# First layer's local attention: a fixed TensorE order in turns 3 to 11, taps in pairs, and 32x32 transposes for norms and reciprocals

## The chip, the cores and the metric

The kernel runs on one core of a Trainium2 chip. The metric is the device time of one execution in microseconds. The engines are called PE (TensorE), DVE (VectorE), ACT (ScalarE), POOL (GpSimd) and SP (the queue that issues all DMAs here); PEld is PE's weight load. All data is fp32.

## The reference

Four image layers are applied to two images of 512 channels and 64x64 pixels, each after a group norm and with a residual. The change lies in the first, a local-plus-pooled attention with 8 heads of 64 channels:

```python
q_norm = _l2norm(q)                                   # per token and head
q_scaled = (q_norm + query_embedding) * softplus(temperature)
k_l = _l2norm(k_l)
attn_local = einsum('bhnd,bhndk->bhnk', q_scaled, k_local)   # 3x3 neighbours: 9 taps
attn_pool = einsum('bhnd,bhpd->bhnp', q_scaled, _l2norm(k_pool))   # 256 pooled keys
attn = softmax(concatenate([attn_local, attn_pool], axis=-1), axis=-1)
a_local, a_pool = attn[..., :9], attn[..., 9:]
lt = einsum('bhnd,hdk->bhnk', q_norm, learnable_tokens) + learnable_bias + a_local
x_local = einsum('bhnk,bhndk->bhnd', lt, v_local)
x_pool = einsum('bhnp,bhpd->bhnd', a_pool, v_pool)
out = (x_local + x_pool) @ W_proj + b_proj
```

## The kernel before, in words

The class `Local` (from line 1938) computes this layer for one image. Channels lie on partitions, 128 at a time, so a chunk of channels holds two heads. A unit is one chunk and 1024 tokens (16 image rows): 4 chunks by 4 blocks of tokens make 16 units. `run` (line 2018) walks through turns i = -4 to 16. One turn works on several units at once, in a software pipeline: it projects the keys of unit i+4 and the queries of unit i+3 (`projections`, line 2255), makes their norms (`norms`, line 2289), multiplies them in one turn later (`normed`, line 2333), forms the tap products and sums of unit i+1 (`tap_products` line 2379, `tap_sums` line 2394), attends for unit i (`attend`, line 2421) and weighs the values of unit i-1 with the nine local probabilities and the pooled part (`weigh`, line 2502). Each stage is a Python generator. `in_turn` runs all of them to their next `yield`, again and again, so a turn is some ten steps in which each stage contributes a piece. Which step a piece stands in fixes the order in which the program is written.

It doesn't fix the order in which the engines run it. The Tile scheduler orders each engine's instructions by priority (the written order) and by when it takes them to be ready, and places the semaphores. PE's queue therefore mixes pieces of neighbouring steps and turns.

PSUM has eight banks. Five of them are a common pool (`bank()`, name `mm`), one holds the tap sums, two hold a PSUM copy of the queries (`qs`).

What the prediction's steps touch:

- **Norms.** At line 2299 four matmuls, each with 32 output rows, sum the squares of the two heads of four streams (two key blocks, two query blocks) into one bank. Line 2302 copies it to SBUF on ACT, line 2306 transposes it on PE in four 128x128 pieces, so that tokens lie on partitions and the 32 useful numbers of a partition are short rows. Lines 2313 to 2321 form 1/sqrt on DVE by three Newton steps, 13 small instructions, into `wide`. At step 5 line 2327 transposes back on PE and line 2329 copies to SBUF. `normed` spreads the two rows of a stream over the channels with a matmul of two rows (line 2341) and multiplies on DVE (line 2349). `learned` (line 2362) then multiplies the queries with the learnable tokens.
- **Taps.** Line 2384 copies the queries to PSUM. For each of nine shifts line 2389 multiplies them with the shifted keys on DVE (128x1024) into one of three buffers, and line 2402 sums over channels on PE: per product and half of the tokens one matmul with 32 output columns, up to four of which lie side by side in the array.
- **Pooled attention.** Line 2434 makes the scores (two heads side by side, 64 rows each), line 2438 the exponentials, line 2444 the weighted pooled values, line 2449 adds the exponentials in pairs on POOL. `sums` (lines 2456 and 2460) forms the denominators at step 7 in a bank in which every row of a head holds the same sums, and line 2481 takes the reciprocal of all 128x512 in two halves on DVE. Lines 2484 and 2485 finish the local probabilities; line 2488 writes them to DRAM at step 8, and line 2500 fetches each tap's row back spread over 64 partitions.
- **Weighing.** For each of ten parts ACT copies the fetched tap into two banks (line 2514), DVE multiplies (lines 2519 and 2522), POOL adds (line 2527). Three tap buffers go round.
- **Projections.** Line 134 (`project`) does four matmuls of 128x128 by 512 for a block. A turn has six such blocks: two keys and two queries at steps 6 to 9, two values at steps 0 and 3.
- `fetch_output` loads W_proj into the four `sq` tiles in turn 13; `output` applies it in the last turns.

Of the kernel before, what the change touches and what calls it, by code (L numbers as in the profile page):

```python
# [9 lines left out]
F32 = mybir.dt.float32  # L10
I32 = mybir.dt.int32
AF = mybir.ActivationFunctionType
ALU = mybir.AluOpType
# [3 lines left out]
P = 128  # L17
# [1920 lines left out]
class Local:  # L1938
# [9 lines left out]
    def __init__(self, net, X, Y, sp_scale, d, wp, yp, pp, ppt, pps):  # L1948
# [20 lines left out]
        self.prods = [whole.take([P, self.UT])] + [new([P, self.UT], f"prod{i}") for i in range(2)]  # L1969
# [19 lines left out]
        self.qn = new([P, self.UT], "qn")  # L1989
# [3 lines left out]
        self.wide = new([P, NT, P], "wide")  # L1993
# [12 lines left out]
        nc.gpsimd.memset(self.wide, 0.0)  # L2006
# [11 lines left out]
    def run(self):  # L2018


        self.nmean = self.net.stats[:, 0]
        xs = self.pooled_tokens()
        heads = self.pooled_heads(xs)
        units = KC * self.UN
        unit = lambda u: u if 0 <= u < units else None
        self.pending = []
        for i in "qkv":
            self.fetch(i, 0)
        for i in range(-4, units + 1):
            k, q, ahead, u, before = (unit(i + n) for n in (4, 3, 1, 0, -1))  # L2030
            streams, ended = [], []
            stages = [self.norms(streams, ended)]
            if ahead is not None:
                stages.append(self.tap_products(ahead))
            if u is not None:
                stages.append(self.attend(u))
            if before is not None:
                stages.append(self.weigh(before))
            if ahead is not None:
                stages.append(self.tap_sums(ahead))  # L2040

            values = ([ahead] if i >= self.UN - 1 and ahead is not None
                      else {-4: [0], -3: [1, 2], -2: [3]}.get(i, []))
            stages.append(self.projections(k, q, values, streams))
            stages.append(self.normed(ended))
            if i < -2:
                stages.append(islice(heads, 12 if i == -4 else None))
            if i == units - 3:
                stages.append(self.fetch_output())
            if i > units - 3:  # L2050
                stages.append(self.output(i - units + 2))
            in_turn(*stages)

        self.nc.sync.dma_start(self.next_w, self.d["w_q1"].rearrange("(kc p) o -> p kc o", p=P))
        in_turn(self.output(KC - 1))
# [136 lines left out]
    def fetch_output(self):  # L2192

        for _ in range(3):

            yield
        for kc in range(KC):
            self.nc.sync.dma_start(self.sq[kc], self.d["W_proj"][kc * P:(kc + 1) * P, :])
        self.pb = self.kp[:, :2, :].rearrange("p c n -> p (c n)")
        self.nc.sync.dma_start(self.pb, self.d["pb_rows"])  # L2200
        yield

    def output(self, c4):
# [4 lines left out]
        toks = ([self.prods[0], self.prods[1], self.prods[2], self.qs[(units - 2) % 3]] if c4 % 2  # L2208
# [46 lines left out]
    def projections(self, uk, uq, uvs, streams):  # L2255
# [22 lines left out]
        values = [(u, j) for u in uvs for j in range(2)]  # L2278
        for step in range(10):
            if step >= 6:  # L2280
                project((uk, uq)[step // 2 - 3], "kq"[step // 2 - 3], step % 2)
            if step % 3 == 0 and values:
                u, j = values.pop(0)
                self.value(u, j)
                if j and self.last(u):
                    self.fetch("v", u // self.UN + 1)
            yield

    def norms(self, streams, ended):
# [11 lines left out]
        rows = wp.tile([P, TB], F32, name="n_rows")  # L2301
        nc.scalar.copy(rows, ps)
        yield
        ps = self.bank()
        for t in range(NT):
            nc.tensor.transpose(ps[:, t * P:(t + 1) * P], rows[:, t * P:(t + 1) * P],
                                self.net.ident)


        sums = ps.rearrange("p (t s r) -> p t s r", t=NT, s=4)  # L2310
        n, a = (sums[:, :, :, 2 * i:2 * i + 2] for i in range(2))
        y = wp.tile([P, NT, 4, 2], F32, name="roots")
# [4 lines left out]
        for i in range(3):  # L2317
            nc.vector.tensor_tensor(a, n, y, ALU.mult)
            nc.vector.tensor_tensor(a, a, y, ALU.mult)
            dst = self.wide.rearrange("p t (s r) -> p t s r", s=4)[:, :, :, :2] if i == 2 else y  # L2320
            nc.vector.scalar_tensor_tensor(dst, a, 1.5, y, ALU.add, ALU.mult)
        yield
        yield
        yield
        ps = self.bank()
        for t in range(NT):
            nc.tensor.transpose(ps[:, t * P:(t + 1) * P], self.wide[:, t, :], self.net.ident)
        rows = wp.tile([P, TB], F32, name="n_rows")
        nc.scalar.copy(rows, ps)
# [3 lines left out]
    def normed(self, ended):  # L2333

        nc = self.nc
        for _ in range(5):
            yield
        for which in "kq":
# [4 lines left out]
            for (_, _, _, u, j, part, _), ps in mine:  # L2343
# [5 lines left out]
                nc.vector.tensor_tensor(out, part, ps, ALU.mult)  # L2349
# [29 lines left out]
    def tap_products(self, u):  # L2379

        qs = self.pps.tile([P, self.UT], F32, name="qs")
        for j in range(2):
            part = slice(j * TB, (j + 1) * TB)
            self.nc.scalar.copy(qs[:, part], self.qs[u % 3][:, part])
        qs = qs.rearrange("p (y x) -> p y x", x=W)
        y = u % self.UN * self.UY
        for k in range(9):
            dy, dx = divmod(k, 3)
            self.nc.vector.tensor_tensor(  # L2389
                self.prods[k % 3].rearrange("p (y x) -> p y x", x=W), qs,  # L2390
                self.kx[:, y + dy:y + dy + self.UY, dx:dx + W], ALU.mult)
            yield

    def tap_sums(self, u):
# [3 lines left out]

        def sums(k):
            for j in range(2):  # L2400
                q = 2 * j + k % 2
                nc.tensor.matmul(ps[32 * q:32 * q + 32, :],  # L2402
                                 self.cst[:, C_TAPW + 16 - 2 * k:C_TAPW + 48 - 2 * k],
                                 self.prods[k % 3][:, j * TB:(j + 1) * TB], start=(k < 2),
                                 stop=(k > 6))

        yield
        yield
        for k in range(0, 8, 2):
            sums(k)  # L2410
            sums(k + 1)
            yield
            if k < 6:
                yield
        sums(8)
# [5 lines left out]
    def attend(self, u):  # L2421
# [5 lines left out]
        prob = {}  # L2427
# [12 lines left out]
        def values(j):  # L2440
# [6 lines left out]
            dst = prob[1, 1] if j else self.halves  # L2447
            for h in range(2):
                nc.gpsimd.tensor_tensor(dst[h], prob[j, 0][h], prob[j, 1][h], ALU.add)  # L2449

        def sums():
            psD = self.bank()
            blocks = [slice(j * HD, (j + 1) * HD) for j in range(2)]
            for h in range(2):
                for j, b in enumerate(blocks):
                    nc.tensor.matmul(psD[b, :], self.cst[:, C_EVEN + h:C_EVEN + h + HD],
                                     (prob[1, 1] if j else self.halves)[h], start=(h == 0),
                                     stop=False)
# [8 lines left out]
        yield  # L2467
        values(0)
        yield
        exponentials(1, 0)  # L2470
        yield
        exponentials(1, 1)
        yield
        values(1)
        yield
        yield
        psD = sums()

        for i in range(2):
            part = slice(i * TB // 2, (i + 1) * TB // 2)  # L2480
            nc.vector.reciprocal(self.recip[:, part], psD[:, part])  # L2481
# [3 lines left out]
        nc.vector.tensor_tensor(el, el, self.lt.pop(u), ALU.add)  # L2485
        self.spread = self.rows()
# [237 lines left out]
```

## Time and profile before

| | |
|---|---|
| median of three runs | 5136.01 us (5133.57 to 5157.94) |
| profiled execution | 5143.42 us, span of its instructions 5141.5 us |
| mean granted TensorE clock | 0.981 |
| PE busy | 4890.5 us, 95% |
| DVE, ACT, POOL busy | 3069.4, 1864.1, 1845.4 us |
| first layer, first image: first and last L2299 group | 196.8 and 859.6 us |
| steady turns 4 to 11, first image | 465.6 to 817.4 us |
| the same, second image | 3017.3 to 3368.3 us |
| DMA fetch of a tap row (L2500), issue to landing | 4.1 us |

An fp32 matmul is recorded as two instructions. Matmuls overlap in PE's pipeline, so the length of a record is more than its share of time: what a group costs is read from its start to the next group's start. In the waits, a line reads: who waited, for whom, total us, times, longest us. The granted clock is the share of full speed that PE's clock was given in the stretch.

### The profile page before, as it was taken

The numbers are of one execution on the slowest core, as the hardware profiler recorded it, in microseconds if no ns is written. First come the engines' busy times: TensorE is split into PE (matmuls) and PEld (weight loads), VectorE is DVE, ScalarE is ACT, GpSimd is POOL, SyncE is SP. The second block draws the span as 40 slices with busy tenths as digits, with TensorE's granted clock in tenths as the row PEclk, the third lists the DMA queues.
The fourth block names the chain that finished last, engine by engine and source line by source line (L and its number), as shares of the span: only waits on it lengthen the run. The fifth ranks groups of instructions, "written<-read, shape, count | busy, mean of one in ns | idle before, by whom it ended". The sixth has DMA issues, their size and how long they took to land. (4 is left out here: it accounts for less than half of the span.)

```text
span 5141.5 us, 48728 instructions
## 1 busy us (share of the span) xinstructions
PE 4890.5 (95%) x17299; PEld 2030.9 (39%) x17299; DVE 3069.4 (60%) x3986; ACT 1864.1 (36%) x3547; POOL 1845.4 (36%) x1216
## 2 busy tenths in 40 slices
PE   7999999899999999999999999998999999999998
PEld 3423332455334444433344333335543344444333
DVE  4267777654579633477732677777446795334766
ACT  1245665334323233322112566652343232333221
POOL 0025566500420045454500455555013201454554
PEclk9999999999999999999999999999999999999999
DMA  3025556600000000111110355565000000000111
GB/s 150 2 74 141 143 139 171 178 28 10 1 1 17 2 1 1 66 58 46 64 62 2 95 137 148 142 170 163 19 10 1 2 15 1 1 1 21 40 46 44
DMA packets 124752, 309.88 MB, mean 60 GB/s; under 512 B 20882, under 2 KB 33682, under 8 KB 122964
## 3 DMA queue, kind: packets, MB, share of 16 engines
q1 hardware_dynamic: 124500, 306.68, 20.7%
q8 instruction: 139, 2.28, 0.2%
q14 instruction: 113, 0.93, 0.1%
HBM read 258.11 MB, written 48.50 MB: 60 GB/s over the span
## 5 line engine op out<-in xcount | busy, mean ns | idle before, releaser
L134 PE MATMUL mm<-big,w 128*128 128x512 f32 x2496 | 1163.9, 611 | 8.6 <-DVE late L2481 8.6
L134 PEld LDWEIGHTS mm<-big,w 128*128 128x128 f32 x2496 | 456.4, 192 | 677.3 <-issue 560.3
L2527 POOL TENSOR_TENSOR late<-late,big 128x1024 f32<-128x1024 f32 x192 | 455.0, 2370 | 199.6 <-DVE big L2522 174.4
L1639 POOL TENSOR_TENSOR big<-big 128x512 f32<-128x512 f32 x224 | 277.5, 1271 | 219.6 <-ACT big L1630 219.6
L2449 POOL TENSOR_TENSOR late<-late 128x512 f32<-128x512 f32 x128 | 160.7, 1275 | 521.3 <-ACT late L2438 499.4
L2522 DVE TENSOR_TENSOR big<-big,mm 128x512 f32<-128x512 f32 x384 | 255.6, 681 | 119.0 <-ACT mm L2514 111.4
L2514 ACT COPY mm<-big 128x512 f32<-128x512 f32 x428 | 244.7, 593 | 170.4 <-DMA big<-rows 127.8
L1630 ACT ACTIVATE big<-mm,ed 128x256 f32<-128x256 f32 x512 | 194.0, 490 | 232.6 <-DVE top L1626 200.3
L2527 POOL TENSOR_TENSOR late<-late,tap 128x1024 f32<-128x1024 f32 x96 | 227.2, 2367 | 100.7 <-DVE tap L2522 96.2
L1442 POOL TENSOR_TENSOR wq<-prob 128x512 f32<-128x512 f32 x48 | 70.8, 1497 | 505.6 <-ACT prob L1439 505.6
L1894 PE MATMUL mm<-k,w 128*128 128x512 f32 x512 | 238.5, 610 | 12.3 <-DVE k L1887 7.4
L1626 DVE TENSOR_REDUCE top<-mm 128x1 f32<-128x512 f32 x256 | 159.0, 683 | 148.2 <-PE mm L1557 148.2
L134 PE MATMUL mm<-big,wq 128*128 128x512 f32 x512 | 233.8, 605 | 2.7 <-ACT off_t L1223 2.7
L2389 DVE TENSOR_TENSOR prod<-qs,big 128x1024 f32<-128x1024 f32 x192 | 230.4, 1215 | 8.8 <-PE tap L2402 6.6
L1604 PE MATMUL mm<-w,big 128*128 128x512 f32 x512 | 235.1, 603 | 0.0
L1195 PE MATMUL mm<-big,wo 128*128 128x512 f32 x512 | 234.7, 604 | 0.0
L1352 PE MATMUL acc<-big,diag 128*128 128x512 f32 x512 | 227.4, 601 | 4.6 <-ACT diag L1357 4.6
L973 POOL TENSOR_TENSOR group_stats<-group_stats,cst 128x1 f32<-128x1 f32 (+1 forms) x20 | 12.1, 622 | 574.4 <-DVE group_stats L972 514.2
L1884 DVE RECIPROCAL psD<-psD 128x512 f32<-128x512 f32 x64 | 215.1, 3361 | 1.9
L2402 PE MATMUL tap<-prod,cst 128*32 128x512 f32 x768 | 198.7, 603 | 8.8 <-DVE prod L2389 7.8
L134 PE MATMUL mm<-big,big 128*128 128x512 f32 x464 | 201.7, 594 | 0.5 <-DVE b_sr L1011 0.5
L1439 ACT ACTIVATE prob<-mm 128x512 f32<-128x512 f32 x256 | 133.0, 602 | 171.6 <-PE mm L1436 171.3
(410 smaller groups left out, 8466.1 us busy)
## 6 DMA issues: line engine op xcount, KB each, us to landing
big<-rows SPq DMA_DIRECT2D x428, 256.0 KB, 4.1
tap<-rows SPq DMA_DIRECT2D x212, 256.0 KB, 4.1
yd<-late SPq DMA_DIRECT2D x32, 512.0 KB, 2.9
lost_all<-lost SPq DMA_DIRECT2D x128, 128.0 KB, 3.0
out<-big SPq DMA_DIRECT2D x64, 256.0 KB, 2.0
big<-in_W_kv SPq DMA_DIRECT2D x8, 1024.0 KB, 8.1
rows<-late SPq DMA_DIRECT2D x64, 128.0 KB, 2.3
big<-yd SPq DMA_DIRECT2D x16, 512.0 KB, 5.2
```

Of the source, the lines that this page charges most:

```text
L134: self.nc.tensor.matmul(ps, w[:, kc, :], X[:, kc, blk * TB:(blk + 1) * TB], start=(kc == 0), stop=(kc == KC - 1))
L1195: nc.tensor.matmul(ps, w[:, kc, oc * P:(oc + 1) * P], att[:, kc, :], start=(kc == 0), stop=(kc == KC - 1))
L1352: nc.tensor.matmul(accs[b], dg, src[:, b * TB:(b + 1) * TB], start=(j == 0), stop=(j == 6))
L1604: nc.tensor.matmul(ps, X[:, kc, lo:lo + P], wv[:, kc, :], start=(kc == 0), stop=(kc == KC - 1))
L1639: nc.gpsimd.tensor_tensor(a, a, part, ALU.add)
L1884: nc.vector.reciprocal(psD, psD)
L1894: nc.tensor.matmul(ps, self.wo[:, kc, oc * P:(oc + 1) * P], qs[:, kc, :], start=(kc == 0), stop=(kc == KC - 1))
L2389: self.nc.vector.tensor_tensor(self.prods[k % 3].rearrange("p (y x) -> p y x", x=W), qs, self.kx[:, y + dy:y + dy + self.UY, dx:dx + W], A ...
L2402: nc.tensor.matmul(ps[32 * q:32 * q + 32, :], self.cst[:, C_TAPW + 16 - 2 * k:C_TAPW + 48 - 2 * k], self.prods[k % 3][:, j * TB:(j + 1) * ...
L2514: nc.scalar.copy(ps, part)
L2522: nc.vector.tensor_tensor(part.rearrange("p (y x) -> p y x", x=W), self.vx[:, y:y + self.UY // 2, dx:dx + W], ps.rearrange("p (y x) -> p y ...
L2527: nc.gpsimd.tensor_tensor(out, out, t, ALU.add)
```

## The change

In turns 3 to 11 of each image (`self.steady`), PE's instructions keep the order in which the program writes them, and the steps are rearranged: key projections at steps 4 and 6, queries at 7 and 8, values at 0 and 2; the k products of `normed` at step 3 instead of 5, `learned` at step 6; the pooled values of the first half one step later, together with the scores that follow; POOL's second half sums before the second pooled values, into `sq[2:]`; the denominators at step 6 instead of 7. The tap products are made two at a time, 2048 elements in one instruction, into two double buffers, and the third pair is queued on DVE behind the last multiplication of `normed`.

In all turns, the sums of squares stay in their PSUM bank: DVE transposes it in 32x32 blocks in place, does the Newton steps on the two useful columns of each block, and transposes back into `sq[1]`. The PE transposes, both ACT copies and `wide` are gone. The reciprocals work likewise: DVE transposes the denominators in place, inverts two columns of each block, and transposes them back, each pair read 16 times.

In all other turns the tap products now go round four single buffers instead of three. `fetch_output` waits seven steps instead of three, since `sq[1]` is in use longer.

```diff
@@ run
+            self.steady = self.UN <= i + 1 and i < units - 4
...
-            in_turn(*stages)
+            if self.steady:
+                with self.net.tc.manual_schedule(engines={mybir.EngineType.PE}):
+                    in_turn(*stages)
+            else:
+                in_turn(*stages)
@@ fetch_output
-        for _ in range(3):
+        for _ in range(7):
@@ projections
+        made, taken = ((4, 6, 7, 8), (0, 2)) if self.steady else ((6, 7, 8, 9), (0, 3, 6, 9))
         for step in range(10):
-            if step >= 6:
-                project((uk, uq)[step // 2 - 3], "kq"[step // 2 - 3], step % 2)
-            if step % 3 == 0 and values:
+            if step in made:
+                i = made.index(step)
+                project((uk, uq)[i // 2], "kq"[i // 2], i % 2)
+            if step in taken and values:
@@ norms
-        rows = wp.tile([P, TB], F32, name="n_rows")
-        nc.scalar.copy(rows, ps)
-        yield
-        ps = self.bank()
-        for t in range(NT):
-            nc.tensor.transpose(ps[:, t * P:(t + 1) * P], rows[:, t * P:(t + 1) * P],
-                                self.net.ident)
-        sums = ps.rearrange("p (t s r) -> p t s r", t=NT, s=4)
-        n, a = (sums[:, :, :, 2 * i:2 * i + 2] for i in range(2))
-        y = wp.tile([P, NT, 4, 2], F32, name="roots")
+        yield
+        nc.vector.transpose(ps, ps)
+        n, a = (ps.rearrange("p (b r) -> p b r", r=32)[:, :, 2 * i:2 * i + 2] for i in range(2))
+        y = wp.tile([P, TB // 32, 2], F32, name="roots")
...
-        yield
-        yield
-        yield
-        ps = self.bank()
-        for t in range(NT):
-            nc.tensor.transpose(ps[:, t * P:(t + 1) * P], self.wide[:, t, :], self.net.ident)
-        rows = wp.tile([P, TB], F32, name="n_rows")
-        nc.scalar.copy(rows, ps)
+        rows = self.sq[1]
+        nc.vector.transpose(rows, ps)
@@ normed
-        for _ in range(5):
+        for _ in range(3 if self.steady else 5):
             yield
...
-                nc.vector.tensor_tensor(out, part, ps, ALU.mult)
+                self.multiplied = nc.vector.tensor_tensor(out, part, ps, ALU.mult).ins
+            yield
+        if self.steady:
             yield
@@ tap_products
+        for k in range(0, 9, 2) if self.steady else range(9):
+            n = min(2, 9 - k) if self.steady else 1
+            held = (self.net.tc.issue_after(self.multiplied) if self.steady and k == 4
+                    else nullcontext())
+            with held:
+                self.nc.vector.tensor_tensor(
+                    self.pair(u, k)[:, :n].rearrange("p k (y x) -> p k y x", x=W),
+                    bcast(qs.rearrange("p (y x) -> p y x", x=W), 1, n),
+                    self.shifted(u % self.UN * self.UY, k, n), ALU.mult)
+            for _ in range(n):
+                yield
+
+    def pair(self, u, k):
+        return self.prods[(5 * u + k // 2) % 2][:, k % 2:]
@@ tap_sums
+        yield
+        if not self.steady:
+            yield
         for k in range(9):
             for j in range(2):
...
+            if k % 2:
+                for _ in range(((2, 2, 3, 1) if self.steady else (2, 2, 2, 1))[k // 2]):
+                    yield
@@ attend
+        def halved(j):
+            if j not in half:
+                half[j] = self.halves if not j else self.sq[2:] if self.steady else prob[1, 1]
+                for h in range(2):
+                    nc.gpsimd.tensor_tensor(half[j][h], prob[j, 0][h], prob[j, 1][h], ALU.add)
...
         exponentials(0, 1)
         yield
+        if self.steady:
+            yield
         values(0)
-        yield
+        if not self.steady:
+            yield
         exponentials(1, 0)
         yield
         exponentials(1, 1)
+        if self.steady:
+            halved(1)
         yield
         values(1)
         yield
-        yield
+        if not self.steady:
+            yield
         psD = sums()
-        for i in range(2):
-            part = slice(i * TB // 2, (i + 1) * TB // 2)
-            nc.vector.reciprocal(self.recip[:, part], psD[:, part])
+        nc.vector.transpose(psD, psD)
+        two = psD.rearrange("p (b n r) -> p b n r", n=16, r=2)[:, :, 0]
+        nc.vector.reciprocal(two, two)
+        nc.vector.transpose(self.recip.rearrange("p (b n r) -> p b n r", n=16, r=2),
+                            bcast(two, 2, 16))
```

## The prediction, made before the changed kernel was run

> **What bounds the kernel.** First the page's busy times, then the first layer cut into turns (from one L2299 group of TensorE, PE, to the next), then PE's timeline inside one turn, then PE's waits.
>
> ```profile
> PE 4890.5 (95%) x17299; PEld 2030.9 (39%) x17299; DVE 3069.4 (60%) x3986; ACT 1864.1 (36%) x3547; POOL 1845.4 (36%) x1216
> ```
> PE is the only engine near its limit. By stretch (columns: busy us with instructions of PE, PEld, DVE, ACT, POOL, then granted clock, DMA share, GB/s):
>
> ```profile
> 196.80:233.30 36.50, 34.43 (x105) 14.96 (x105) 6.51 (x24) 8.57 (x14) 3.39 (x3) 0.95 0.00 0
> 257.90:291.40 33.50, 31.00 (x108) 10.04 (x109) 15.02 (x26) 12.03 (x18) 0.00 (x0) 0.95 0.03 8
> 371.70:421.50 49.80, 45.61 (x160) 14.11 (x162) 35.36 (x55) 26.77 (x47) 26.22 (x13) 0.97 0.53 144
> 465.60:817.40 351.80, 350.09 (x1285) 117.04 (x1284) 256.39 (x401) 214.71 (x376) 209.23 (x104) 1.00 0.55 143
> ```
> The last row is turns 4 to 11, eight of the nine that get the fixed order: 43.98 us each (43.88 in the second image), PE busy 99.5%; turn 3 is counted like them. The clean turns among them take 43.60. The others are filling turns with waits and a lower clock. In a steady turn, starts on PE:
>
> ```profile
> 598.92 1.13 PE L2434 MATMUL mm<-big,kp 64*128 64x512 f32 x4
> ...
> 600.97 0.66 PE L2306 MATMUL mm<-cst,n_rows 128*128 128x128 f32 x4
> 601.56 1.94 PE L2444 MATMUL mm<-late,vp 128*64 128x512 f32 x8
> 603.43 1.35 PE L2434 MATMUL mm<-big,kp 64*128 64x512 f32 x4
> ...
> 611.38 0.66 PE L2327 MATMUL mm<-cst,wide 128*128 128x128 f32 x4
> 611.97 1.94 PE L2444 MATMUL mm<-late,vp 128*64 128x512 f32 x8
> 613.84 1.13 PE L2341 MATMUL mm<-n_rows,cst 2*128 2x512 f32 x4
> 614.89 3.70 PE L134 MATMUL mm<-big,w 128*128 128x512 f32 x8
> 618.53 1.13 PE L2341 MATMUL mm<-n_rows,cst 2*128 2x512 f32 x4
> ...
> 626.98 1.02 PE L2402 MATMUL tap<-prod,cst 128*32 128x512 f32 x2
> 627.94 4.56 PE L134 MATMUL mm<-big,w 128*128 128x512 f32 x10
> ```
> Start to start gives each group's price; one fp32 matmul is two records. The L2402 group at 626.98 is one product alone: 0.96 us, as much as four side by side. PE's waits between 196.8 and 421.5 (us in total, times, longest):
>
> ```profile
> PE mm L2327 <- DVE wide L2321: 4.6, 3, 2.0
> PE tap L2402 <- DVE prod L2389: 2.5, 6, 1.4
> PE mm L2341 <- ACT n_rows L2329: 2.3, 3, 0.8
> PE mm L2306 <- ACT n_rows L2302: 1.1, 2, 0.8
> ```
>
> **1. Norms without PE transposes, all turns.** L2306 and L2327 go: 0.59 + 0.59 = 1.18 us of PE a call, 34 calls (136 records each, four a call): 40.1 us, of which 18 steady turns hold 21.2 and the 16 others 18.9. Two ACT copies go (2 x 0.58), hidden anyway. Two DVE transposes of 128x512 come. No such row exists; the nearest is a transposing reduction of the same size, and a plain PSUM copy L2160 (0.69) bounds it below:
>
> ```profile
> L1822 DVE TRANSPOSE_TENSOR_REDUCE sq_cols<-sq x64: 654/699/714, 2158.7 to 5081.1; 128x16 f32<-128x512 f32 x64
> L2481 DVE RECIPROCAL late<-mm x64: 1694/1724/1758, 312.3 to 3537.2; 128x256 f32<-128x256 f32 x64
> ```
> (Columns: ns, least/median/most.) I take 0.70. [...] DVE (256.4/8 = 32.05 a turn) stays below PE, so the work moves off the bound engine[...].
>
> **2. Fixed order, pairs, early denominators (18 turns).** The lone product rejoins its three companions: -0.96. Three neighbours of equal tile shape get separated: L2362 then pays its own change of shape (+0.1), the ninth product stands alone (+0.14), and sixteen L134 records in a row become two groups of 3.64 (+0.2). Net -0.5. A clean turn: 43.60 - 1.18 - 0.5 = 41.9.
>
> DVE: nine products of 1.22 become four of 2048 elements and one of 1024. From 0.68 at 512 and 1.22 at 1024, 2048 costs 2.29: 10.94 becomes 10.4. With the reciprocal (3) DVE has 32.05 + 1.40 - 0.6 - 1.7 = 31.2 a turn, POOL 26.2, ACT 25.7: all hidden behind 42, if the order lets them.
>
> Whether it does, I checked along the traced order, from a turn's start (E = L2434, V/P = L134, N = L2299, T = L2402, A = L2444, n = L2341). E V ends at 4.7; N to 5.7; E T V to 11.4; A E T to 15.5; then n(k). The norm chain is 2 x 0.70 + 13 small steps of 0.19 = 3.9 of its own; before, it took 602.82 to 609.96, 7.1, so 4.6 of other DVE work lay inside. N's end + 3.9 + 4.6 = 14.3: 1.2 before n(k). If a pair of 2.29 falls into it where a single one did, the slack is about nothing. The pair at the fifth product is queued behind n(k)'s multiplications: 16.6 + 2 x 0.69 + 2.29 = 20.3 against its T at 24; behind it DVE's weighing waits as well, so ACT's copies and, through the tap buffers, POOL; some 4 us cover that. The denominators at 25 need POOL's half sums: exponentials end near 19, at most one addition of 2.36 ahead, two of 1.27: 23.9, covered by about 1 us. The SP queue: tap rows and fetches stay in their steps; W_proj's loads slip four steps ahead of turn 13's rows (4.7 us to landing), at worst 5 us an image, needed a turn later.
>
> Not in the trace is how PSUM's five banks fit. A, E, n, E lie close together, 1+2+2+2 banks, beside the two that weighing holds. Before, E behind A already took up to 1.35. The second E can wait for n's two multiplications: 0 to 1.7. With the chain, new waits are 0 to 3 us a turn. No excess work can appear on PE, so below zero is excluded. I take 0.6, nearest to the 0.33 that steady turns lose now (43.93 - 43.60), since DVE, ACT and POOL all have a quarter to spare. Turn: 42.5, so 1.43 x 18 = 26 us.
>
> **Filling turns.** Transposes 18.9. The waits above on the norm chain are 4.6 + 2.3 + 1.1 = 8.0 an image. The clock: (1 - 0.95) x 36.5 + (1 - 0.95) x 33.5 + (1 - 0.97) x 49.8 = 1.8 + 1.7 + 1.5 = 5.0 us lost. [...] the trace grants less in just these turns, so I count 13 an image. The chain passed five engines' work (0.59 + 0.59 + 2.5 + 0.59 + 0.58 = 4.9 and four handovers), now 3.9 and two. Bounds 0 to 26 for both images; I take half, 13.
>
> **3. Reciprocals, 32 calls.** 2 x 1.73 = 3.45 becomes two transposes and a reciprocal of 32 elements (0.2 at 8 elements, 6.3 ns each more: 0.35): 1.75, so -1.7 of DVE. In steady turns no wait of PE ends on it. In the last four turns PE waits for L2481 4.3 an image, and the last unit's weighing starts 1.7 earlier. Bounds 0 to 12, less W_proj's slip; I take 6.
>
> **Sum.** 26 + 18.9 + 13 + 6 = 64. The profiled execution took 5143.4 (span 5141.5), so it would take 5079; the median of the three timed runs, 5136.0, lies 7.4 below it, and the same 64 off that gives 5072.
>
> **Rivals.** (a) No new waits at all: turns of 41.9 (2.03 x 18 = 36.5), filling 18.9 + 26, tail 10: 91, so 5045. For it: all other engines have room. Against: E behind A waits now. 0.15. (b) The fixed order loses its gain: the scheduler could let late taps slide behind other groups, a fixed order waits. With 2 us of waits a turn stays 43.9; 38 is left: 5098. For it: the slacks of 0 to 1 us above. 0.22. (c) Slower: five banks. If E, n(q) and A each wait for a bank freed only behind a 2.29 us pair on DVE, PE loses some 2 us three times, 6 a turn: 47.9, so +72 - 38, 5170. It turns slower from turns of 43.93 + 38/18 = 46.0, waits of 4.1. Against: before, weighing and E shared the same banks with 0.3 lost. 0.06. (d) Between b and c, waits of 3 to 4: about 5125, 0.07. The main case keeps 0.50.
>
> **Numbers.** 5072. The range 5043 to 5112 takes in (a) and (b) and leaves out (c), (d) and the edges. About 0.5% (26 us) is what measurement tells from no change here: faster 0.83, same 0.11, slower 0.06.
>
> **What would show it.** Right: L2306 and L2327 gone, steady turns 42 to 43, taps in groups of eight records, DVE transposes near 0.70, granted clock 0.97 or more in the filling turns. Wrong: turns at 44 with PE waiting for DVE before L2402 or L2341, or for ACT and DVE before the second L2434 (banks); transposes well above 0.70, which would lengthen both chains.

## The result, and the profile after

The changed kernel took 5100.6 us (median of five runs, 5097.1 to 5108.0), the kernel before on the same chip 5145.0 (5133.6 to 5158.0): ratio 0.992, interval 0.9904 to 0.9935, about 44 us less. The profiled execution took 5100.1 us with a span of 5098.3, 43.2 below the span of before. The forecast was 64.

First the page's busy times, then the stretches that answer to those of before: turn -3, turn -1, turn 2, turn 3 and turns 4 to 11 of the first image.

```profile
PE 4835.1 (95%) x17027; PEld 1992.3 (39%) x17027; DVE 3067.0 (60%) x4014; ACT 1817.9 (36%) x3479; POOL 1843.8 (36%) x1214
```

```profile
194.20:230.30 36.10, 35.14 (x93) 14.67 (x92) 7.83 (x26) 7.47 (x12) 3.39 (x3) 0.91 0.00 0
253.50:285.80 32.30, 29.65 (x100) 9.30 (x99) 16.34 (x28) 10.83 (x16) 0.00 (x0) 0.95 0.03 9
365.30:411.10 45.80, 41.83 (x134) 13.51 (x129) 28.91 (x49) 24.68 (x44) 26.08 (x13) 0.93 0.45 126
411.10:456.50 45.40, 42.92 (x153) 13.44 (x152) 33.24 (x51) 26.43 (x47) 26.18 (x13) 1.00 0.61 163
456.50:797.80 341.30, 335.71 (x1219) 105.45 (x1218) 256.42 (x394) 202.24 (x360) 209.37 (x104) 1.00 0.54 148
```

Turn 3 of the kernel before, for comparison:

```profile
421.50:465.60 44.10, 43.38 (x157) 14.35 (x156) 30.15 (x49) 26.61 (x47) 26.13 (x13) 1.00 0.49 134
```

Three things are to be seen. Turns 4 to 11 took 341.3 instead of 351.8; turns 4 to 10 are 42.54 each, in both images, with 0.7 of waits. The three filling turns shown are shorter, but their clock is 0.91 to 0.95, no higher than before (0.95 to 0.97). And turn 3, the first with the fixed order, takes 45.4 (45.8 in the second image), where before it took 44.2 (43.7).

The whole difference, between first L2299 (now L2303) groups, both images together:

| stretch | before | after | difference |
|---|---|---|---|
| turns -3 to 2 | 453.2 | 434.5 | -18.7 |
| turn 3 | 87.8 | 91.2 | +3.4 |
| turns 4 to 11 | 702.8 | 682.6 | -20.2 |
| turn 12 | 85.3 | 86.7 | +1.4 |
| all the rest | | | -9.1 |
| span | 5141.5 | 5098.3 | -43.2 |

PE's timeline in a steady turn (L2408 are the taps, L2330 is n, L2433 the scores, L2443 the pooled values):

```profile
587.45 3.70 PE L134 MATMUL mm<-big,w 128*128 128x512 f32 x8 [0.17 <-ACT late L2437]
...
594.00 1.06 PE L2408 MATMUL tap<-prods,cst 128*32 128x512 f32 x8
595.00 1.13 PE L2330 MATMUL mm<-sq,cst 2*128 2x512 f32 x4
596.06 1.13 PE L2433 MATMUL mm<-big,kp 64*128 64x512 f32 x4
597.71 3.70 PE L134 MATMUL mm<-big,w 128*128 128x512 f32 x8 [0.53 <-DVE big L2338]
601.34 1.13 PE L2330 MATMUL mm<-sq,cst 2*128 2x512 f32 x4
```

All taps stand in groups of eight records but the ninth product's four. The two waits left are for PSUM banks: a projection (L134) waits 0.17 for one that the exponentials (L2437) hold, and the first key projection 0.53 for the one that n's multiplication (L2338) holds. PE's waits in turns -3 to 2 of the first image, and DVE's new operations:

```profile
PE mm L2330 <- DVE sq L2318: 5.2, 3, 2.5
PE mm L134 <- DVE big L2534: 2.4, 1, 2.4
PE tap L2408 <- DVE prods L2381: 1.7, 7, 0.4
```

```profile
L2306 DVE STREAM_TRANSPOSE mm<-mm x34: 722/731/732, 195.4 to 3374.3; 128x512 f32<-128x512 f32 x34
...
L2318 DVE STREAM_TRANSPOSE sq<-mm x34: 707/716/717, 199.1 to 3382.7; 128x512 f32<-128x512 f32 x34
...
L2489 DVE RECIPROCAL mm<-mm x32: 351/366/367, 306.8 to 3500.0; 128x32 f32<-128x32 f32 x32
```

PE still waits for the norm chain, 5.2 us instead of the 8.0 that its three waits made before: n (L2330) waits for the chain's last transpose (L2318). The transposes cost what was taken (0.73 and 0.72 for 0.70), the reciprocal 0.37 for 0.35.

### The profile page after: what moved, and what is told of

It reads as the page before. It is cut to its first block, busy times and chain, and to the rows that moved or that the text cites. A ratio compares the mean times of both kernels' runs of the same rounds, so it can differ in the third digit from the quotient of the medians.

```text
span 5098.3 us, 48031 instructions
## 1 busy us (share of the span) xinstructions
PE 4835.1 (95%) x17027; PEld 1992.3 (39%) x17027; DVE 3067.0 (60%) x4014; ACT 1817.9 (36%) x3479; POOL 1843.8 (36%) x1214
## 5 line engine op out<-in xcount | busy, mean ns | idle before, releaser
L134 PE MATMUL mm<-big,w 128*128 128x512 f32 x2496 | 1178.8, 616 | 33.0 <-DVE big L2338 9.5
L134 PEld LDWEIGHTS mm<-big,w 128*128 128x128 f32 x2496 | 458.0, 193 | 717.8 <-issue 560.1
L2381 DVE TENSOR_TENSOR prods<-qs,big 128x1024 f32<-128x1024 f32 (+1 forms) x216 | 335.3, 1569 | 66.4 <-PE tap L2408 56.2
L2452 POOL TENSOR_TENSOR late<-late 128x512 f32<-128x512 f32 x92 | 115.4, 1274 | 440.3 <-ACT late L2437 416.7
L134 PE MATMUL mm<-big,wq 128*128 128x512 f32 x512 | 232.2, 602 | 2.7 <-ACT off_t L1223 2.7
L1884 DVE RECIPROCAL psD<-psD 128x512 f32<-128x512 f32 x64 | 215.1, 3361 | 1.9
L134 PE MATMUL mm<-big,big 128*128 128x512 f32 x464 | 201.7, 594 | 0.5 <-DVE b_sr L1011 0.5
L2408 PE MATMUL tap<-prods,cst 128*32 128x512 f32 x1152 | 195.3, 604 | 5.1 <-DVE prods L2381 4.3
```

Source lines behind the costliest of these rows:

```text
L134: self.nc.tensor.matmul(ps, w[:, kc, :], X[:, kc, blk * TB:(blk + 1) * TB], start=(kc == 0), stop=(kc == KC - 1))
L1884: nc.vector.reciprocal(psD, psD)
L2381: self.nc.vector.tensor_tensor(self.pair(u, k)[:, :n].rearrange("p k (y x) -> p k y x", x=W), bcast(qs.rearrange("p (y x) -> p y x", x=W), ...
L2408: nc.tensor.matmul(ps[32 * q:32 * q + 32, :], self.cst[:, C_TAPW + 16 - 2 * k:][:, :32], self.pair(u, k)[:, 0, j * TB:(j + 1) * TB], start ...
```

## The experiments

Theory 1, from the prediction: what is taken off PE is time, 1.18 us a call, and the fixed order adds half a microsecond a turn; the parts add up. Its rival: the parts depend on each other, and the scheduler's order turns freed PE time into waits and split groups (matmuls that could lie side by side in the array, as the eight tap records in 1.06 us at 594.00, but run one behind the other).

All kernels compute the whole reference. Ratios are to the runs of the kernel before on the same chip (medians from 5138.0 to 5145.0), with 95% intervals. "Steady" is the mean of turns 4 to 10, first image; "filling" is turns -3 to 2, first and second image; the last column is turn 3 likewise.

| kernel | median us | ratio | steady | filling | turn 3 |
|---|---|---|---|---|---|
| before | 5145.0 | 1 | 44.02 | 224.7, 228.5 | 44.2, 43.7 |
| changed | 5100.6 | 0.992 (0.9904 to 0.9935) | 42.54 | 216.9, 217.5 | 45.4, 45.8 |
| no_steady | 5118.5 | 0.9955 (0.994 to 0.9969) | 43.96 | 216.5, 216.6 | 44.5, 44.1 |
| steady_auto | 5174.0 | 1.0068 (1.0055 to 1.008) | 46.33 | 215.5, 215.9 | 47.8, 47.7 |
| order_only | 5156.5 | 1.0036 (1.0024 to 1.0048) | 44.49 | 223.4, 220.3 | 46.0, 48.5 |
| old_recip | 5104.6 | 0.9931 (0.9918 to 0.9944) | 42.54 | 214.3, 218.3 | 46.4, 46.6 |
| fill_old_norms | 5110.3 | 0.9931 (0.9916 to 0.9947) | 42.54 | 221.0, 220.8 | 46.6, 47.2 |
| steady_old_norms | 5131.5 | 0.9982 (0.9974 to 0.999) | 44.58 | 214.1, 217.1 | 48.2, 47.8 |
| singles | 5086.5 | 0.989 (0.9874 to 0.9906) | 42.54 | 213.7, 215.6 | 42.5, 42.5 |
| from2 | 5092.3 | 0.9903 (0.9887 to 0.9918) | 42.54 | 217.4, 215.4 | 42.5, 42.5 |
| three_bufs | 5102.9 | 0.9929 (0.9912 to 0.9946) | 42.54 | 214.8, 216.5 | 46.5, 45.5 |
| late_denoms | 5134.7 | 0.9991 (0.9983 to 0.9999) | 44.42 | 215.1, 217.6 | 46.5, 45.6 |
| singles_key5 | 5125.0 | 0.9969 (0.9959 to 0.9978) | 44.74 | 213.3, 217.1 | 42.7, 42.7 |
| weigh_last | 5119.5 | 0.9961 (0.995 to 0.9971) | 43.96 | 214.8, 215.5 | 43.7, 43.6 |

PE's time by group in a steady turn (start to start, waits ahead of a group apart; the records overlap: in turns 4 to 11 of the changed kernel's first image an L134 record is 605 ns on average, and a group of eight 3.70 us):

| kernel | L134 | taps | scores | pooled | denominators | n | transposes | squares, learned | waits |
|---|---|---|---|---|---|---|---|---|---|
| before | 21.59 | 5.78 | 4.56 | 3.78 | 2.87 | 2.12 | 1.18 | 1.90 | 0.24 |
| changed | 21.79 | 5.04 | 4.31 | 3.74 | 2.87 | 2.12 | 0 | 2.00 | 0.70 |
| no_steady | 21.59 | 6.09 | 4.77 | 3.90 | 2.87 | 2.30 | 0 | 1.88 | 0.55 |
| steady_auto | 22.51 | 6.88 | 4.31 | 3.73 | 2.87 | 2.92 | 0 | 1.88 | 1.23 |
| order_only | 21.79 | 4.94 | 4.38 | 3.81 | 2.87 | 2.12 | 1.24 | 1.88 | 1.47 |
| steady_old_norms | 21.75 | 4.97 | 4.31 | 3.74 | 2.87 | 2.12 | 1.05 | 2.00 | 1.78 |
| late_denoms | 22.14 | 5.10 | 5.05 | 3.74 | 2.87 | 2.12 | 0 | 2.00 | 1.42 |

**no_steady: the norms and reciprocals alone (and the fourth tap buffer).**

```diff
-            self.steady = self.UN <= i + 1 and i < units - 4
+            self.steady = False
```

> Turns 3 to 11 go back to the scheduler's order, single tap products and late denominators; norms and reciprocals stay on DVE in all turns. Theory 1 (the steady gain is mostly the PE transposes taken away, 1.18 us a turn; fixed order, pairs and early denominators add only about 0.2 net and cost a transition): steady turns 42.5 to 43.0 against 42.54 in the changed kernel, no slow turn 3, total 5096 to 5110. Rival (the scheduler cannot use the freed PE time because DVE's longer queue delays n and the taps; the fixed order is what turns it into time): steady turns 43.5 or more, total 5118 to 5130.

Steady turns stayed at 43.96 (44.02 before), the rival's side; the total, 5118.5, is at its edge. The transposes are gone, and the freed 1.18 is spent again, line by line in the table: taps +0.31, scores +0.21, pooled +0.12, n +0.18, waits +0.31. PE's timeline of one of its turns shows how (the number after the start is the group's length):

```profile
3049.13 1.66 PE L2433 MATMUL mm<-big,kp 64*128 64x512 f32 x4 [0.22 <-DVE mm L2314]
...
3056.40 1.05 PE L2408 MATMUL tap<-prods,cst 128*32 128x512 f32 x2
...
3060.96 3.70 PE L134 MATMUL mm<-big,w 128*128 128x512 f32 x8 [0.28 <-DVE big L2534]
...
3073.03 1.57 PE L2408 MATMUL tap<-prods,cst 128*32 128x512 f32 x8
```

A lone tap (two records in 1.05), a tap group that takes 1.57 where eight records can take 1.06, scores of 1.66 instead of 1.13, and 0.22 and 0.28 of waits for DVE. That DVE's longer queue causes this, the rival's reason, is not shown: DVE is busy 31.6 us a turn here, 32.05 before. The whole gain of this kernel lies outside turns 4 to 11.

**steady_auto: the new steps, pairs and early denominators, the order left to the scheduler.**

```diff
-            if self.steady:
-                with self.net.tc.manual_schedule(engines={mybir.EngineType.PE}):
-                    in_turn(*stages)
-            else:
-                in_turn(*stages)
+            in_turn(*stages)
```

> The changed kernel with its steps, pairs and early denominators, but PE's order left to the scheduler. Theory 1 (the fixed order saves the lone tap and costs the waits at turns 3 and 12): the lone tap comes back, +0.3 to +0.7 a steady turn, turn 3 loses its 1.7 us wait; total between -3 and +9 against the changed kernel. Rival (the fixed order carries the gain): steady turns 43.5 and more, +18 or more.

The rival held, and by far: turns of 46.33, and 73 us above the changed kernel where it said 18 or more. Taps take 6.88; L134 is longer by 0.9, near the estimated 0.9 that the clock costs (one minus the granted 0.98 of turns 4 to 11, times their 370.8 us, over eight turns; 1.00 was granted before: see the last section); n takes 2.92, because the two matmuls of its first group run one behind the other (1.93 instead of 1.13); waits are 1.23. The new steps without the fixed order are worse than nothing.

**order_only: before, with PE's order fixed as written in turns 3 to 11.** The `manual_schedule` block above, put into the kernel before.

> The kernel before with PE's order fixed as written in turns 3 to 11, nothing else changed. Theory 1 (order alone is worth about 0.5 a turn where nothing waits, but the old steps were not laid out for it): steady turns 43.3 to 45.0 against 43.93, total within 15 us of the kernel before, waits in front of the second transposes and the denominators. Rival (the order by itself is the gain): steady turns 42.6 or less, total -20 or lower.

44.49 a turn as theory 1 said, the total 3.5 us beyond its bound. The order does mend the groups (taps -0.84, scores -0.18 a turn), but waits rise from 0.24 to 1.47: 0.74 a turn for a bank held by the exponentials, the rest for n's rows and for ACT.

**steady_old_norms: fixed order, pairs, early denominators, with the old norms in turns 3 to 11.** `norms` of before, its three yields between the two transposes cut to one.

> The changed kernel with the norms of before in the steady turns: fixed order, pairs and early denominators stay, two groups of PE transposes and two ACT copies come back. Theory 1 (under a fixed order the two groups cost their 1.18 us a turn, and the chain through ACT and PE makes n later): steady turns 43.7 to 45.0, total +21 to +45. Rival (the fixed order and the steps alone make the gain, the transposes fill waits of 0.7): steady turns below 43.3, total below +14.

44.58 and 31 us above the changed kernel, as theory 1 said: 1.05 of transposes, and 1.26 of waits in front of the second one. With these steps the fixed order needs the short norm chain.

**late_denoms: the denominators at step 7 again.**

```diff
         values(1)
         yield
-        if not self.steady:
-            yield
+        yield
         psD = sums()
...
         nc.vector.tensor_tensor(el, el, self.lt.pop(u), ALU.add)
-        if self.steady:
-            yield
```

> The changed kernel with the denominators at step 7 again in turns 3 to 11 (order fixed, pairs kept, norms on DVE). Theory 1 (the denominators are covered either way, the step only moves the weighing of the next turn): steady turns 42.5 to 42.9, total -2 to +8. Rival (the weighing then starts too late, its banks come free late and PE waits before the scores, as in turn 3 of the changed kernel): 1 to 3 us a turn, total +18 to +50.

The rival held: turns of 43.1 to 48.2, 34 us more than the changed kernel. Scores grew from 4.31 to 5.05 and waits from 0.70 to 1.42, of these 0.76 L134 waiting for a bank that the exponentials hold. The scores' growth is a wait too, and the one that the rival named. In each of the 16 turns 4 to 11 the second matmul of the first scores group starts some 0.05 us after DVE ends the first product of the weighing (L2528), and so behind the first matmul instead of beside it. While the first one's record lasts, the profile shows no idle time. L134 grew by 0.35; over turns 4 to 11 of the first image the granted clock is 0.99, in the changed kernel 1.00. One step later for the denominators costs 1.9 a turn, more than the whole change gains there (1.48).

**old_recip: the two reciprocals of 128x256 back.**

```diff
-        nc.vector.transpose(psD, psD)
-        two = psD.rearrange("p (b n r) -> p b n r", n=16, r=2)[:, :, 0]
-        nc.vector.reciprocal(two, two)
-        nc.vector.transpose(self.recip.rearrange("p (b n r) -> p b n r", n=16, r=2),
-                            bcast(two, 2, 16))
+        for i in range(2):
+            part = slice(i * TB // 2, (i + 1) * TB // 2)
+            nc.vector.reciprocal(self.recip[:, part], psD[:, part])
```

> The changed kernel with the two reciprocals of 128x256 in place of two transposes and one reciprocal of 32 elements: DVE +1.7 us a call, 32 calls. Theory 1 (in steady turns DVE has 10 us to spare and no PE wait ends on the denominators; only the last turns of an image feel them): steady turns 42.5 to 42.7, total +2 to +6. Rival (fixed order made PE sensitive to every DVE delay): 1 us or more a steady turn, total +18 or more.

Steady turns unchanged at 42.54, DVE at 33.3 us a turn instead of 32.05, hidden. The total is 4.0 higher, inside theory 1's 2 to 6, but the intervals of the two ratios overlap.

**fill_old_norms: the old norms in the 16 calls outside turns 3 to 11.** The mirror image of steady_old_norms, with all three yields.

> The changed kernel with the norms of before (PE transposes, two ACT copies) in the 16 calls outside turns 3 to 11. Theory 1 (in the filling turns every PE instruction taken away is time, because PE waits little there): turns -3 to 2 longer by 12 x 1.18 = 14 us in the two images together, total +14 to +19. Rival (as in the steady turns under the scheduler's order, the freed PE time comes back as waits and split groups): total 0 to +6.

Between the two: the filling turns are 7.4 longer together (14 were expected there), the medians 9.7 apart, and the two ratios' intervals overlap. In the filling turns of the first image PE shows transposes +7.4 and waits +3.5, but taps 22.4 instead of 25.4: over a quarter of the old norms' cost comes back as better grouped taps. Part of the rest is the clock. One minus the granted clock, times the length, gives 20.4 us of loss in these filling turns and 23.8 in those of the changed kernel; without it they are some 11 longer, nearer to theory 1. So it isn't settled between the two.

**three_bufs: three single tap buffers outside turns 3 to 11.**

```diff
     def pair(self, u, k):
-        return self.prods[(5 * u + k // 2) % 2][:, k % 2:]
+        if self.steady:
+            return self.prods[(5 * u + k // 2) % 2][:, k % 2:]
+        i = (9 * u + k) % 3
+        return self.prods[i // 2][:, i % 2:]
```

> The changed kernel with three single tap buffers again, instead of four, in the turns outside 3 to 11. Theory 1 (in turns -3 to 2 the fourth buffer lets the scheduler keep four products side by side: taps cost 25.4 us of PE an image there, 32.1 before): taps rise by 4 to 7 us an image, total +8 to +14. Rival (the taps group better because the norms no longer lie between them): taps within 1.5 us of 25.4 an image, total within 3 us.

The rival: taps 26.7 an image, total 2.3 apart. With three buffers n waits less (3.6) and the taps more (4.3 instead of 1.7), which balances. The taps' fall in the filling turns from 32.1 to 25.4 comes with the new norms and without the fourth buffer; with the old norms and four buffers it came as well (22.4). But order_only, with neither, has 28.5, and no_steady, with both, 28.2: the scheduler regroups the taps with any change near by, and which part of the change does it isn't settled.

**singles: tap products one at a time in all turns.**

```diff
-        for k in range(0, 9, 2) if self.steady else range(9):
-            n = min(2, 9 - k) if self.steady else 1
+        for k in range(9):
+            n = 1
```

> The changed kernel with the tap products one at a time in turns 3 to 11 (nine of 1.22 us for four of 2.29 and one of 1.22; PE's order unchanged). Theory 1 (DVE's 0.6 us a turn lies beside PE, which has 10 us over it): steady turns 42.4 to 42.8, total within 4 us of the changed kernel. Rival (pairs keep DVE's queue short where PE waits for taps): 0.5 us or more a turn, total +9 or more.

Neither: steady turns are the same, and the kernel is faster, ratio 0.989 against 0.992 (differences of spans: 14.3 us). Turn 3 falls from 45.4 and 45.8 to 42.5, turn 2 from 45.8 and 45.9 to 44.1. So the pairs cause the slow turn 3. Its wait is `PE mm L2433 <- DVE late L2531`, 1.6 us: the scores want a bank that the first product of the weighing holds. The scores' second matmul then runs behind the first instead of beside it, which costs another 1.1 (5.42 of scores where a steady turn has 4.31). That product starts at 414.04 in the changed kernel, at 407.90 with singles. The queue that issues the DMAs (SP) shows why, in the changed kernel and then in singles (L2500 writes the probabilities, L2512 fetches the rows, L2545 writes the result of the unit before):

```profile
402.39 1.10 SPq L2500 DMA_DIRECT2D rows<-late  x2
407.91 0.33 SPq L2545 DMA_DIRECT2D yd<-late  x1
408.41 1.11 SPq L2512 DMA_DIRECT2D tap<-rows  x2
```

```profile
399.30 1.10 SPq L2500 DMA_DIRECT2D rows<-late  x2
402.33 1.10 SPq L2512 DMA_DIRECT2D tap<-rows  x2
403.53 1.18 SPq L2512 DMA_DIRECT2D big<-rows  x2
405.95 0.33 SPq L2545 DMA_DIRECT2D yd<-late  x1
```

DVE in the changed kernel, and then in singles (L2381 are the tap products):

```profile
395.23 0.37 DVE L2489 RECIPROCAL mm<-mm 128x32 f32<-128x32 f32 x1
395.50 2.27 DVE L2381 TENSOR_TENSOR prods<-qs,big 128x2048 f32<-128x2048 f32 x1
...
399.49 2.28 DVE L2381 TENSOR_TENSOR prods<-qs,big 128x2048 f32<-128x2048 f32 x1
401.69 0.68 DVE L2495 TENSOR_TENSOR late<-late 128x512 f32<-128x512 f32 x1
```

```profile
394.26 0.37 DVE L2489 RECIPROCAL mm<-mm 128x32 f32<-128x32 f32 x1
394.54 1.21 DVE L2381 TENSOR_TENSOR prods<-qs,big 128x1024 f32<-128x1024 f32 x1
...
396.29 1.19 DVE L2381 TENSOR_TENSOR prods<-qs,big 128x1024 f32<-128x1024 f32 x1
...
398.59 0.68 DVE L2495 TENSOR_TENSOR late<-late 128x512 f32<-128x512 f32 x1
```

Two pairs of turn 3 (2.27 and 2.28 us) are taken up already in turn 2, between the reciprocal and the last step of the probabilities (L2495), where the single products are 1.21 and 1.19: the rows leave 3.1 us later (1.0 of it was there before the reciprocal). And the first fetch now stands behind L2545, which waits 4.3 us for POOL's last addition. 3.1 late on DVE become 6.1 late on SP.

**from2: the steady form from turn 2.**

```diff
-            self.steady = self.UN <= i + 1 and i < units - 4
+            self.steady = self.UN <= i + 2 and i < units - 4
```

> The changed kernel with the steady form from turn 2 instead of turn 3. Theory 1 (turn 3 is slow, 45.4 and 45.8, because turn 2's late denominators make its weighing late): turn 3 falls to 42.5 to 43.5, turn 2 (45.8) stays or falls, total -3 to -10. Rival (the step from the scheduler's order to the fixed one costs its 3 us wherever it lies): turn 2 rises by what turn 3 loses, total within 2 us.

Turn 3 falls to 42.5 as theory 1 said, but turn 2 rises from 45.8 and 45.9 to 49.0 and 46.9, with PE waiting 7.7 and 6.7 us for exponentials. By the turns the rival is nearer (a net gain of 1.9 in turns 2 and 3), by the ratio theory 1 (0.9903, interval overlapping with 0.992); it isn't settled, since the same filling turns differ by up to 4 us between the two images of one execution.

**singles_key5: singles, and the first key projection at step 5.**

```diff
-        made, taken = ((4, 6, 7, 8), (0, 2)) if self.steady else ((6, 7, 8, 9), (0, 3, 6, 9))
+        made, taken = ((5, 6, 7, 8), (0, 2)) if self.steady else ((6, 7, 8, 9), (0, 3, 6, 9))
```

> Single tap products in all turns, and in turns 3 to 11 the first key projection at step 5 instead of 4. Theory 1 (its 0.53 us wait is for a bank that n's multiplication holds, and one step later the bank is free): steady turns 42.0, 18 x 0.53 = 9.5 us off the kernel with single products. Rival (the next group in the queue needs the bank instead, and what the projection covered is now bare): steady turns 42.5 or more, no gain, up to +20.

The wait moved to the next group, as the rival said, with the same 0.52. But the turns are 42.7 to 46.3, and the total is 39 us above singles, beyond the rival's 20. It is not the waits, which stay 0.70:

```profile
599.76 2.05 PE L2330 MATMUL mm<-sq,cst 2*128 2x512 f32 x4 [0.52 <-DVE big L2338]
601.74 3.68 PE L2443 MATMUL mm<-late,vp 128*64 128x512 f32 x8
605.36 1.94 PE L2408 MATMUL tap<-prods,cst 128*32 128x512 f32 x8
```

The three groups take nearly twice their 1.13, 1.94 and 1.06. The granted clock is 0.93 over this turn, which takes 46.1, and 1.00 over the next one, which takes 42.7.

**weigh_last: singles, the weighing written behind n's multiplications.**

```diff
-            if before is not None:
-                stages.append(self.weigh(before))
...
             stages.append(self.normed(ended))
+            if before is not None:
+                at = 1 + (ahead is not None) + (u is not None)
+                stages.insert(len(stages) if self.steady else at, self.weigh(before))
```

> Single tap products in all turns, and in turns 3 to 11 the weighing written behind n's multiplications of the same step, so that DVE takes n's products first; PE's order stays the same. Theory 1 (the 0.53 us wait of the first key projection is for a bank whose n product stands on DVE behind a weighing product that itself waits 0.9 for ACT's copy): the wait falls to 0.2 or less, steady turns 42.2, total -4 to -8 against the kernel with single products. Rival (weighing gives its two banks back later, and PE waits for those): steady turns 42.6 or more, total 0 to +30.

The wait of the key projection is gone, as theory 1 said, and so is the gain, as the rival said: turns of 43.96, and 33 us above singles, a little beyond its 30. Scores take 5.15 instead of 4.31: in turns 4 to 10 of the first image the second matmul of the scores group ahead of the projection starts just after n's multiplication ends (597.50 and 597.54 in one turn), so the bank's wait has moved there. A projection waits up to 0.80 for a bank of the weighing, the pooled values 0.30 for ACT. The best version found is singles.

## Why the prediction held, and where its size was off

The sign and the steady turn were right, and the time lay in the range. Of the 64 us, 21 were lost in three terms. The 5072 missed by 29: the other 9 are its base, a median of three runs, 5136.0, where five gave 5145.0.

**Steady turns.** 42.5 was predicted, 42.54 measured in turns 4 to 10. Inside, against the first image's 44.02: transposes -1.18 as predicted; regrouping -0.5 predicted, -0.76 measured (taps -0.74, scores -0.25, L134 +0.20, others +0.03); waits 0.24 to 0.70, +0.46, where the sum put 0.6 in place of the 0.33 of a mean turn, +0.27. So the turn came out exact because two misses, -0.26 and +0.19, nearly cancel. The new wait is for a bank at n's multiplications, as named, but at the key projection behind the second scores group instead of at that group, with a third of the price (0 to 1.7) at which it was bounded. What the prediction did not see is that these parts don't add: with the norms alone a turn stays at 43.96 (no_steady); everything but the fixed order gives 46.33 (steady_auto), everything but the norms 44.58 (steady_old_norms), everything but the early denominators 44.42 (late_denoms): each of the last three is slower than before. That the denominators at step 6 are "covered by about 1 us" held: PE never waits for them in a steady turn. What step 6 is worth the prediction did not see: one step later, the weighing gives back its banks too late.

**The 18th part: turn 3.** The sum counted 18 equal turns at 1.43. Turn 3 went +1.3 and +2.1 instead of -1.43 each, and turn 11 ends at 43.52: the 26 became 16.8. Of the 9.2 lost, 6.2 are turn 3 and the rest mostly turn 11. The step that failed is "turn 3 is counted like them". The prediction did name what happens, a pair of 2.29 us ahead of somebody in DVE's queue, but looked for it in the steady state, where there is slack, and not where the scheduler's order meets the fixed one. singles shows it: without pairs turn 3 takes 42.5.

**Filling turns.** The transposes were right, some -14 in 12 calls. The half of "waits and clock", 13, was not: waits fell by 1.5 together, not by 8 or more. The chain got shorter, but n still waits 5.2 us an image for it, and a new wait of 2.4 for a bank of the weighing came. The clock did not come back either: the sign named was 0.97 or more, and the turns shown have 0.91 to 0.95. One minus the granted clock, times the length, was 15.3 us in both images before and 23.8 after. In eight other kernels with the new norms in these turns it is 17.0 to 22.1, in order_only, with the old ones, 13.6, but in fill_old_norms, with the old ones too, 20.4. So it came back in no kernel, it scatters by several us, and that the new norms make it worse is not shown. Against that, the taps regrouped (-6.7 an image), which the prediction had not looked at in these turns. Net: 18.7 where about 27 was counted for these 12 calls. Without the clock it would have been an estimated 27.2, but that agreement is luck: half of it is taps, not waits.

**The rest.** Four calls (4.7) and 6 for the reciprocals were counted; turn 12 at +1.4 and the rest at -9.1 make 7.7. But this is not a measurement of them: the rest holds the other layers too, and over the fourteen profiles its three stretches (ahead of the first norms, between the images' turns 13 and -3, behind the last turn 13) scatter by 3, 9 and 10 us. Nor do the waits show the reciprocals' 6: L134's waits for them, 8.6 us in both images, are gone, but in the last turns it now waits 8.7 for ACT (L2356, the bias on `learned`'s product). That the reciprocals don't matter in the steady turns is shown by old_recip (42.54 as well), whose total of +4.0 is within the noise of two medians.

**Rivals.** (c), slower by banks, did not occur in the changed kernel, but its mechanism is real: against the changed kernel's 42.54, late_denoms and weigh_last lose 1.9 and 1.4 a turn, most of it to such waits, shown as idle time or hidden in the scores. (b) came true for turn 3 alone.

**DVE.** 31.2 us a turn was predicted and 32.05 measured, as before. Summed by instruction, DVE's work in turns 4 to 11 of the first image fell from 34.6 to 34.2 a turn, half of the 0.85 counted; 0.27 of the other half is one step of the probabilities (L2494), which takes 0.95 instead of 0.68. The busy time counts overlapping instructions once, and fewer overlap now. It lies under PE either way. The new transposes of 128x512 take 0.73 and 0.72 us. steady_old_norms, with the transposes on PE, takes 2.0 us a turn more (44.58 against 42.54).

## What to carry to other kernels

When one engine is bound, taking work off it gains time only where the order of the rest lets its neighbours close up: test the removal, the order and the step of what comes next together and one by one. Here the removal alone gained 0.06 in a steady turn and the order alone lost 0.47; the new steps alone, and the third pair's place in DVE's queue, were not tried. Look for the price of a bigger instruction or a new order where the old order ends and the new begins, and follow the delay from queue to queue (3.1 us on DVE were 6.1 on SP). The bank wait moved by hand came back at another group both times (singles_key5: 0.52 ahead of n; weigh_last: scores of 5.15 instead of 4.31); count what is queued behind before moving it.

## What was not expected of the hardware

In singles_key5 PE was slower behind a single wait of half a microsecond; in the changed kernel and in singles, with waits of up to 0.5 in every turn 4 to 11, it was not. In the turn shown for singles_key5, the groups behind the wait of 0.52 ahead of n take 2.05, 3.68 and 1.94 us instead of 1.13, 1.94 and 1.06. The granted clock over this turn (586.2 to 632.3) is 0.93, over the next one (632.3 to 675.0) 1.00.

Turns 4 to 11 of the first image, with some of PE's waits (total us, times, longest us):

| kernel | waits of PE | granted clock |
|---|---|---|
| before | n for its rows: 1.3, 3, 0.6 | 1.00 |
| changed | L134 for n's multiplication: 4.2, 8, 0.5 | 1.00 |
| singles (waits of turns 3 to 11) | L134 for n's multiplication: 4.7, 9, 0.5 | 1.00 |
| order_only | L134 for the exponentials: 5.9, 8, 0.7; n for its rows: 2.8, 7, 0.6 | 1.00 |
| steady_old_norms | second transposes for the roots: 10.1, 8, 1.3 | 1.00 |
| late_denoms | L134 for the exponentials: 5.7, 8, 1.5; for n's multiplication: 4.2, 8, 0.5 | 0.99 |
| steady_auto | L134 for n's multiplication: 5.7, 8, 0.7; taps for their products: 2.3, 7, 0.3 | 0.98 |
| singles_key5 | n for n's multiplication: 0.52 in the turn shown | 0.96 |

A wait of up to 1.3 in every turn goes with 1.00 in steady_old_norms, and one of up to 0.7 with 0.98 in steady_auto. Waits of up to 0.6 ahead of n go with 1.00 in order_only, and one of 0.52 with 0.93 in the turn of singles_key5. So neither the length of a wait nor the group behind it tells these turns apart, and what does is not shown by these runs.
